# A hybrid of window attention, linear attention and a recurrence: the second image's channel blocks in the planner's list

## The chip, the cores and the metric

The kernel runs on one NeuronCore of a Trainium2 chip. A core has five engines that run their own instruction streams: TensorE (PE in the profile, with its weight loads as PEld), VectorE (DVE), ScalarE (ACT), GpSimd (POOL) and SyncE (SP). SP does no arithmetic here; it issues nearly all DMA transfers, in order. [...] The metric is device time in microseconds of one execution.

## The reference

The input is 16 images of 56 x 56 pixels with 128 channels, in float32. Layer 0 normalises each image by groups of channels and runs shifted window attention on 7 x 7 windows (64 windows per image, 4 heads of 32). Layer 1 takes each image as 3136 tokens, runs causal linear attention, and then a recurrence over the tokens. Cut to what matters:

```python
x = x + window_attention(_gn(x), w_qkv, pos_emb, w_out, b_out)  # 7x7 windows
t = _to_tokens(x)                                  # (16, 3136, 128)
t = t + linear_attention(_ln_t(t), W, b)           # causal, running k-v state
wx = batch_norm(_ln_t(t) @ ffn_W.T)                # mean and variance over all images
for i in range(3136):                              # one state per image
    y[:, i] = sigmoid(wx[:, i] + y[:, i - 1] @ V.T)
t = t + y
```

`_gn` needs the mean and variance of a whole image before its first window can be projected. The recurrence needs the statistics of all images, so it comes last.

## The kernel before

**Two parts.** The first part works through the images one after another and overlaps neighbouring ones. Its instruction order is computed by a small planner in the kernel. The second part, the recurrence, has an order written by hand (from about 1497 us on in the profiled execution).

**One image in the first part.** An image is loaded twice. `load` (L323 issues it) brings its tokens into `xt_buf`, tokens on partitions, in seven groups: six of 512 tokens and one of 64. `load_turned` brings the same image into `spare[0]` as four channel blocks of 32 channels, through `load_blocks` (L335); block q fills partitions 32q to 32q+31. Seven 32 x 32 block transposes on DVE (`turn_rows`, L683) turn `spare[0]` into channels on partitions in `xw_buf`; each reads all 128 partitions, so all four blocks. Seven `bn_stats` on DVE (L755) follow, then the group norm: two small matmuls (L784, L800), a few tiny DVE and POOL steps, and a wrap-around copy of the borders on POOL (L773, L774). The first image is turned by TensorE instead (L649), from `xt_buf`.

Then come eight rows of windows. A row is gathered and normalised by ACT (L851), projected (L864, L885), scored (L909, in 32-row matmuls), masked and reduced on DVE (L920, L932), shifted on POOL (L935), exponentiated on ACT (L945), summed on DVE (L949, L951), scaled on POOL (L954), transposed (L964, copied by ACT in L974) and multiplied with the values (L983, 32-row matmuls again).

After enough rows, the token groups: output bias on POOL (L1223), output projection (L1234, L1243), token norm (L1090 on DVE, L1097 to L1111 on POOL), a trip through DRAM that turns blocks (stored in L1058, read back in L1072, turned on DVE in L1139), features (L1269, L1279, L1288, L1292), values (L1317, L1326), products (L1372, L1382), keys (L1348), running state and outputs (L1401, L1404, L1412, copied by ACT in L1424), the residual (L1482, L1490), a second norm and the input of the recurrence (L1502, L1519).

**The planner.** Each piece of work is a step: an engine, a cost (how long the engine is held), a lag (when its users may start), a rank, the steps it comes after, and the buffers that it takes and gives back. `Plan.forwards` places steps engine by engine, taking the ready step of lowest rank; `Plan.backwards` does the same from the end and gives new ranks. `Plan.emit` alternates them 200 times, keeps the plan with the shortest planned span, and emits all steps in the order of their planned starts. So one changed step can change the order of everything. The steps exist only while the program is built: on the chip, an engine waits only where an instruction uses data or a buffer that another one is still working on.

**Around the change.** The steps of `load_turned` are on SP, with a cost of 2.4 and a lag of 12.0 for the images of index 1 and 2 and of 7.0 for the later ones. Each comes after `issued` (a step without instructions that stands for the loads of constants, with a lag of 19.0) and after the block before it, and all take the one buffer `spare`. The tokens of the image of index 2 are held back by small memsets on POOL (`touch`, L601), which come after the transposes of the second image.

## Time and profile before

| what | value |
|---|---|
| median of 3 runs | 1659.49 us (1656.48 to 1663.47) |
| profiled execution | 1664.5 us |
| its span | 1661.4 us |
| PE busy | 1615.4 us |
| DVE busy | 1398.1 us |
| POOL busy | 1272.0 us |
| ACT busy | 1183.5 us |
| moved by DMA | 322.03 MB, mean 194 GB/s |

The profile is of one execution. Its span is what the engines' records cover; the execution's own time is a little longer. Times within it are counted from the start of the span. A line in order of time gives the start, the length, engine, line, operation and tiles, how many instructions were merged, and in brackets how long the engine had been idle and what ended that. For a DMA on SP the length is that of issuing it. A busy PE need not be at its peak, since matmuls are pipelined.

### The profile page before, as it was taken

How to read it: one execution, taken by the hardware profiler on the slowest of the kernel's cores; microseconds unless marked ns; L12 is line 12 of the kernel's file. 1: busy time of each engine (PE TensorE's matmuls, PEld its weight loads, DVE VectorE, ACT ScalarE, POOL GpSimd, SP SyncE). 2: the span in 40 equal slices, each digit the busy share in tenths (PEclk: the TensorE clock that was granted, in tenths of full speed). 3: DMA queues.
4: the chain of work that ended last, by engine and by line, in shares of the span. 5: the costliest groups of instructions: out<-in, count | busy, mean ns of one | idle time of the engine just before them, and what ended most of it. 6: DMA issues, size and time to landing. Idle time of an engine off the chain costs nothing.

```text
span 1661.4 us, 63385 instructions
## 1 busy us (share of the span) xinstructions
PE 1615.4 (97%) x25458; PEld 1308.8 (79%) x25459; DVE 1398.1 (84%) x3044; ACT 1183.5 (71%) x3156; POOL 1272.0 (77%) x2154
## 2 busy tenths in 40 slices
PE   7899999999999999999999999999999999999997
PEld 6678787887878887878888778878888887876876
DVE  5779987897989888987979798978898786757997
ACT  5577776777777777777677777767677776766765
POOL 6788978897989898888989889878889786770000
PEclk9999999999999999999999999999999999999999
DMA  5486767677677768586766777776755655558999
GB/s 137 109 186 158 192 151 172 187 167 208 154 204 166 199 153 206 149 208 169 194 165 156 204 168 196 167 191 156 196 148 155 159 160 147 190 183 342 403 419 379
DMA packets 776720, 322.03 MB, mean 194 GB/s; under 512 B 400481, under 2 KB 760161, under 8 KB 774625
## 3 DMA queue, kind: packets, MB, share of 16 engines
q1 hardware_dynamic: 774832, 317.10, 69.9%
q8 instruction: 202, 3.31, 0.9%
q10 hardware_dynamic: 1584, 0.79, 0.2%
q14 instruction: 102, 0.83, 0.2%
HBM read 171.54 MB, written 146.24 MB: 191 GB/s over the span
## 4 chain that ended last, share of the span: by engine, by line
PE 69%; POOL 8%; DVE 7%; SPq 5%; DMA 5%; issue 3%; ACT 2%; DVEq 0%; POOLq 0%; ACTq 0%
PE bank L864 8%; PE bank L1269 8%; PE bank L885 5%; PE pair L909 5%; PE state_bank L1412 4%; PE pair L964 4%; PE pair L1401 4%; PE bank L1317 4%; PE pair L1404 4%; PE bank L1502 4%; PE bank L1372 4%; PE pair L983 4%; SPq L1072 4%; PE bank L1234 4%; PE z_buf L1785 2%
## 5 line engine op out<-in xcount | busy, mean ns | idle before, releaser
L954 POOL TENSOR_TENSOR p_buf<-p_buf,rc 128x784 f32<-128x784 f32 x128 | 194.4, 1519 | 42.7 <-DVE rc L951 14.2
L1269 PE MATMUL bank<-xnT,awc_sb 128*128 128x512 f32 (+1 forms) x448 | 212.9, 557 | 3.3 <-DVE xnT L1139 2.7
L935 POOL TENSOR_TENSOR s<-s,mx 128x784 f32<-128x784 f32 x128 | 192.2, 1502 | 30.8 <-DVE mx L932 28.5
L1279 ACT ACTIVATE r<-bank,bqk_neg 128x512 f32<-128x512 f32 (+1 forms) x224 | 143.4, 640 | 76.9 <-PE bank L1269 67.3
L1412 PEld LDWEIGHTS state_bank<-v_buf,k 128*128 128x128 f32 x768 | 125.4, 191 | 52.1 <-issue 26.7
L1292 DVE SCALAR_TENSOR_TENSOR f<-bank,bqk_one,r 128x512 f32<-128x512 f32 (+1 forms) x224 | 147.5, 658 | 12.6 <-ACT r L1288 12.1
L1412 PE MATMUL state_bank<-v_buf,k 128*128 128x129 f32 x768 | 155.4, 284 | 1.3 <-ACT state L1424 1.1
L974 ACT COPY pT<-pair 128x904 f32<-128x904 f32 x128 | 118.7, 927 | 51.0 <-PE pair L964 41.3
L1401 PE MATMUL pair<-state,f 128*128 128x129 f32 x768 | 153.1, 281 | 0.6 <-issue 0.6
L1424 ACT COPY state<-state_bank 128x129 f32<-128x129 f32 x384 | 107.0, 279 | 65.5 <-PE state_bank L1412 63.9
L1401 PEld LDWEIGHTS pair<-state,f 128*128 128x128 f32 x768 | 123.4, 192 | 37.0 <-issue 21.8
L920 DVE TENSOR_TENSOR s<-pair,wmask_sb 128x784 f32<-128x784 f32 x128 | 122.7, 958 | 34.2 <-PE pair L909 30.0
L909 PEld LDWEIGHTS pair<-kT,q_buf 32*49 32x49 f32 x8192 | 106.4, 121 | 41.9 <-issue 15.7
L949 DVE TENSOR_REDUCE sm<-p_buf 128x16 f32<-128x784 f32 x128 | 121.6, 950 | 18.6 <-ACT p_buf L945 18.3
L1223 POOL TENSOR_TENSOR xt_buf<-xt_buf,bout_sb 128x512 f32<-128x512 f32 (+1 forms) x112 | 129.1, 1158 | 10.7 <-DMA xt_buf<-in_x_dram 10.5
L1788 ACT ACTIVATE y_a<-z_buf,bsh 128x256 f32<-128x256 f32 (+1 forms) x218 | 103.0, 473 | 47.4 <-PE z_buf L1785 43.3
L1288 ACT ACTIVATE r<-r 128x512 f32<-128x512 f32 (+1 forms) x224 | 131.9, 589 | 2.4
L1785 PE MATMUL z_buf<-y_a,fvT_sb 128*128 128x256 f32 (+1 forms) x432 | 131.0, 389 | 0.4 <-ACT y_a L1788 0.4
L909 PE MATMUL pair<-kT,q_buf 32*49 32x49 f32 x8192 | 122.8, 206 | 2.8 <-issue 2.4
L964 PE MATMUL pair<-ident,p_buf 113*128 113x113 f32 x1024 | 120.9, 261 | 3.1 <-POOL p_buf L954 2.8
L964 PEld LDWEIGHTS pair<-ident,p_buf 113*128 113x128 f32 x1024 | 107.5, 142 | 20.5 <-issue 11.2
L932 DVE TENSOR_REDUCE mx<-s 128x16 f32<-128x784 f32 x128 | 121.5, 949 | 0.9
(170 smaller groups left out, 4697.1 us busy)
## 6 DMA issues: line engine op xcount, KB each, us to landing
x_d<-xt_buf SPq DMA_DIRECT2D x96, 256.0 KB, 2.6
xt_buf<-in_x_dram SPq DMA_DIRECT2D x93, 256.0 KB, 3.2
spare<-in_x_dram SPq DMA_DIRECT2D x60, 392.0 KB, 4.5
xs_d<-staged SPq DMA_DIRECT2D x15, 1568.0 KB, 6.9
xna_d<-spare SPq DMA_DIRECT2D x90, 256.0 KB, 2.7
xnk_d<-f SPq DMA_DIRECT2D x90, 256.0 KB, 3.0
xnf_d<-spare SPq DMA_DIRECT2D x90, 256.0 KB, 2.8
spare<-xna_d SPq DMA_DIRECT2D x256, 64.0 KB, 2.1
```

What stands on the lines that cost most here:

```text
L864: nc.tensor.matmul(d[key], wqkv_sb[:, j * P : (j + 1) * P], xk, start=True, stop=True)
L909: nc.tensor.matmul(sc[64 * hh : 64 * hh + WT, hp, w * WT : (w + 1) * WT], qT[r : r + HD, w * WT : (w + 1) * WT], d["kT"][r : r + HD, w * W ...
L935: nc.gpsimd.tensor_tensor(d["sf"], d["sf"], d["mx"].unsqueeze(2).to_broadcast([P, nb, WT]), ALU.subtract,)
L954: nc.gpsimd.tensor_tensor(prf, prf, d["rc"].unsqueeze(2).to_broadcast([P, nb, WT]), ALU.mult)
L964: nc.tensor.transpose(pt[:, hp, w2, 0:NQ2], pr[0:NQ2, hp, 2 * w2 : 2 * w2 + 2, :].rearrange("p w k -> p (w k)"), ident[0:NQ2, 0:NQ2],)
L1269: nc.tensor.matmul(d[f"p{j}"], awc_sb[:, j * P : (j + 1) * P], d["xT"][:, :nt], start=True, stop=True,)
L1279: nc.scalar.activation(d[f"r{j}"], d[f"p{j}"], AF.Relu, bias=bqk_neg[:, j : j + 1], scale=-1.0,)
L1288: nc.scalar.activation(d[f"r{j}"], d[f"r{j}"], AF.Exp, scale=-1.0)
L1292: nc.vector.scalar_tensor_tensor(d[key][:, :nt], d[f"p{j}"], bqk_one[:, j : j + 1], d[f"r{j}"], ALU.add, ALU.max,)
L1401: nc.tensor.matmul(to, chunk(d["f0"], cc), t["states"][c], start=True, stop=False)
L1412: nc.tensor.matmul(t["pd"], d["k"][:, cc, :], v1[:, cc, :], start=c == 0, stop=True, skip_group_check=True,)
L1785: nc.tensor.matmul(z, fvT_sb, y_prev, start=False, stop=True, skip_group_check=True)
```

## The change

The list of steps that a channel block comes after no longer holds the block before it, if the image is the second one (index 1). For all later images the list is as it was. All four blocks of the second image still come after `issued` and still take the same buffer.

```diff
                         2.4,
                         rank + q,
                         lambda q=q: load_blocks(b, spare[0], q),
-                        [issued, *parts[-1:]],
+                        [issued, *(parts[-1:] if b > 1 else [])],
                         takes=[buf],
                         lag=12.0 if b < 3 else 7.0,
                     )
```

## The prediction

> **What bounds the kernel now.** I read the page's first two parts, then busy time by stretches, then the instructions of SP, DVE and PE in order of time up to 110 us, and last what PE waits for. The page says which engine is full and whether it is full everywhere:

> ```profile
> PE 1615.4 (97%) x25458; PEld 1308.8 (79%) x25459; DVE 1398.1 (84%) x3044; ACT 1183.5 (71%) x3156; POOL 1272.0 (77%) x2154
> ...
> PE   7899999999999999999999999999999999999997
> ```

> PE has work in all slices but the first two and the last. Busy time by stretches puts numbers on it (columns: stretch, its length, then busy time and instructions of PE, weight loads, DVE, ACT and POOL; granted clock, DMA share, GB/s):

> ```profile
> 0.00:55.00 55.00, 44.95 (x851) 35.54 (x852) 31.13 (x53) 31.51 (x79) 39.76 (x57) 1.00 0.48 118
> 55.00:60.00 5.00, 3.50 (x142) 2.98 (x140) 3.32 (x5) 3.14 (x8) 4.10 (x9) 1.00 0.38 82
> 60.00:64.00 4.00, 3.63 (x12) 2.65 (x13) 1.74 (x7) 1.78 (x3) 3.75 (x8) 0.58 0.21 57
> 64.00:100.00 36.00, 32.03 (x500) 25.15 (x498) 31.22 (x71) 21.58 (x54) 26.48 (x51) 1.00 0.75 180
> 100.00:200.00 100.00, 98.48 (x1778) 79.91 (x1778) 92.69 (x206) 75.25 (x200) 89.88 (x143) 1.00 0.75 176
> 200.00:1400.00 1200.00, 1188.19 (x20148) 966.25 (x20148) 1028.51 (x2304) 876.93 (x2395) 1031.25 (x1738) 1.00 0.70 175
> ```

> The reader is to see that from 200 to 1400 us PE stands idle for 11.8 us in 1200 us: there the kernel is bound by PE's own work, which the change leaves as it is. What a change of the order can win lies in the fill: 10.1 us idle before 55, 1.9 from 55 to 64 (plus slow matmuls at clock 0.58), 4.0 from 64 to 100, 1.5 from 100 to 200.

> Now the loads themselves, on SP, and the first use of them on DVE:

> ```profile
> 11.73 0.43 SPq L335 DMA_DIRECT2D spare<-in_x_dram  x1
> 12.21 5.91 SPq L323 DMA_DIRECT2D xt_buf<-in_x_dram  x7
> 18.17 3.80 SPq L335 DMA_DIRECT2D spare<-in_x_dram  x2
> 48.11 0.39 SPq L1058 DMA_DIRECT2D xna_d<-spare  x1
> 50.52 2.02 SPq L1072 DMA_DIRECT2D spare<-xna_d  x4
> 52.58 0.43 SPq L335 DMA_DIRECT2D spare<-in_x_dram  x1
> ...
> 49.85 0.97 DVE L920 TENSOR_TENSOR s<-pair,wmask_sb 128x784 f32<-128x784 f32 x1 [3.59 <-PE pair L909]
> 68.16 1.16 DVE L683 STREAM_TRANSPOSE xw_buf<-spare 128x448 f32<-128x448 f32 x2
> ```

> Three blocks of the second image are issued by 22 us. The fourth stands behind work of the first image in SP's order and goes out at 52.58; it lands 4.3 us later (the median from issue to landing in that window), about 56.9. Its users on DVE come at 68.16, with no wait before them: they stand there because the planner put them there. Blocks two and three go out in one stretch of 3.80 us, though their landing takes 6.7 us: on the chip no block waits for another. So the change removes no wait of the chip. It removes three waits of 12 us from the planner's list, and everything follows from the order that the planner then writes.

> PE meanwhile runs dry, and the first matmul of the second image's windows is the one at 90.88:

> ```profile
> 58.45 0.94 PE L1234 MATMUL bank<-wout_sb,oT_buf 128*128 128x128 f32 x7 [0.90 <-issue]
> 60.37 1.81 PE L1269 MATMUL bank<-xnT,awc_sb 128*128 128x512 f32 x2 [0.98 <-DVE xnT L1139]
> 79.21 1.16 PE L1372 MATMUL bank<-f,f 128*128 128x128 f32 x8 [0.72 <-DVE f L1292]
> 90.88 0.82 PE L864 MATMUL bank<-oT_buf,wqkv_sb 128*128 128x392 f32 x2
> ```

> **The change part by part.** The built order of the changed kernel shows four moves.

> *SP.* All four blocks go out together right behind the constants, ahead of the seven loads of the second image's tokens. Three loads of 392 KB move before them: at the 250 GB/s or so of 20 to 22 us that delays the tokens by 4.7 us. The last of them now lands about 23 us; their first user on POOL starts at 31.62 without a wait, and DMA is silent from 26 to 32 us, so this costs nothing; without that cover it would cost 4.7 us. The third image's token loads, from 69.88 to 85.6 before, now stand before the read-back of the first normalised group (issued at 50.52 before), and wait on small POOL memsets that the order places after the softmax step which ran at 48.04. I put that read-back 2 us later; its user on DVE came at 59.53, some 5 us after landing, which covers it. The third image's blocks stay chained.

> [...]

> *DVE.* The seven transposes (L683, 0.61 us each), seven statistics (L755, 0.60) and the group-norm steps (1.0 together) move from 68 to 86 us up to the stretch from 36 to 58: 9.5 us. DVE's idle time there (lines with 2.60, 1.50, 1.45, 1.05, 3.59, 0.38 and 1.85 between 30 and 58 us) is 12.4 us, so most is hidden. Not all: walked through by these durations, the softmax maximum of row 3 ends 2.2 us later, but POOL, which uses it, is busy until 0.45 us after its old start; one round on, POOL's scaling of row 3 (52.16) starts 1.2 us late, and PE's transposes of it (53.73) with it. Bounds: 0 if all hides, 4.3 (seven transposes) if none of them does; I take **+1.2 us**, from the walk.

> *PE.* The order is the same through the transposes at 53.73. After it the second image's first projection is 14 groups of matmuls on instead of 44; I put it at 67 us instead of 90.9. From there window rows stand between the token groups, so the waits on DVE and ACT have other work to cover them: the 4.0 us of 64 to 100 go, **-4.0 us**. Bounds: -7.4 (with the 1.9 of 55 to 64 and the 1.5 after 100) and 0. The idle stretch at 57 to 60 stays, since the first image's rows are then spent and the second's not begun. With it stays the slow clock: L1269 takes 1.81 us at 60.37 against 1.02 elsewhere, granted clock 0.58 over 4 us, a loss of 1.7 us; I take 0, bounds -1.7 and +1.7.

> [...]

> *The order beyond 100 us.* All of it is rewritten. One countable thing: PE changes between the 32-row matmuls (L909, L983) and the full ones 406 times instead of 424. Across such a change a start-to-start step is 0.32 us where it is 0.22 otherwise (1408.67 to 1408.99 against 1412.47 to 1412.69). 18 x 0.10 = **-1.8 us**, bounds -3.6 and 0. What can't be counted is how many stalls the new order has. The 24 stretches of 50 us between 200 and 1400 idle 0 to 2.94 us each, mean 0.49, spread 0.82; so a sum over 24 scatters by 4.0, and the difference of two such plans by 5.7. I take 0; bounds -11.8 (no stall left) and +11.8 (twice as many). From 1500 us on the order is written by hand and stays.

> Sum: +1.2 - 4.0 - 1.8 = **-4.6 us**. The profiled execution took 1664.5 us (span 1661.4), 0.3% above the median of 1659.49; its span would become 1656.8, and from the median I get **1655 us**, 0.3% less.

> **The rivals.**
> 1. *The fill is lost again.* The inserted DVE work costs its whole 4.3 us against 4.0 and 1.8 won: 1658. For it: POOL is 88% busy from 20 to 40 us and DVE's idle time comes in pieces of 1 to 3 us.
> 2. *The new order is better throughout.* Fill and clock at their bounds without the part after 100 (-5.9, -1.7), changes -1.8, one spread of stalls -5.7: 1644. For it: DVE and POOL are idle for 14% of the time after 200. Against: only 1% of PE is left to win there.
> 3. *Slower: late feedback in the steady part.* One such place before: PE waits 2.7 us for DVE at 1384.9, and clock 0.5 follows for 3.4 us, 4.4 us in all.

> ```profile
> 1387.56 1.34 PE L1317 MATMUL bank<-awc_sb,xnT 128*128 128x128 f32 x8 [2.69 <-DVE xt_buf L1243]
> ```

> Each further such place costs 4.4 us; three outweigh the gain by 8.6 us, which is where it decides: 1668. For it: SP issues in order, and the new order puts more loads with waits before read-backs. Against: only two stretches of 24 hold such a place now.

> **How the numbers follow.** What can be told from no change is about 0.5%, 8.3 us. Chances: forecast 0.40, rival 1 0.15, rival 2 0.27, rival 3 0.18. Faster by over 0.5% is rival 2 and the forecast's lower edge (0.05): 0.32; slower is rival 3: 0.18; the rest 0.50. The likeliest case alone spans 1649 to 1661. The range reaches to both outer rivals and a little beyond the slower one, whose stalls have no ceiling: 1643 to 1671.

> **What would show it.** Right: L683 on DVE near 37 to 46 us, the second image's L864 before 70 us, PE idle from 64 to 100 under 1.5 us, 200 to 1400 near 12. Wrong: L1269's first pair later than 62 us, PE idle in the steady part over 20 us, or clock below 1.00 in more than the two stretches there.

## The result and the profile after

The changed kernel takes 1665.91 us (median of 12 runs, 1660.24 to 1674.23) against 1656.97 us for the kernel before (12 runs, 1655.40 to 1663.47). The ratio is 1.0048, with an interval from 1.0031 to 1.0066. It is 0.48% slower where 0.3% faster was forecast; the time lies inside the range, the direction is wrong. The profiled execution took 1666.84 us, with a span of 1665.1.

The page of the changed kernel again says what is full:

```profile
PE 1615.3 (97%) x25459; PEld 1306.4 (78%) x25459; DVE 1398.8 (84%) x3044; ACT 1185.8 (71%) x3156; POOL 1271.2 (76%) x2154
...
PE   7999999999999999999999999999999999999997
```

PE is busy for 1615.3 us, as before (1615.4). The work is the same; only the idle time and the slow clock can have moved. Busy time by stretches, with the columns of before (stretch, length, then PE, weight loads, DVE, ACT, POOL; granted clock, DMA share, GB/s):

```profile
0.00:55.00 55.00, 45.13 (x885) 35.90 (x889) 38.02 (x71) 31.93 (x79) 40.48 (x66) 1.00 0.63 153
55.00:60.00 5.00, 4.29 (x128) 3.58 (x118) 4.28 (x8) 2.79 (x8) 4.75 (x9) 1.00 0.73 140
60.00:64.00 4.00, 4.00 (x143) 2.91 (x142) 2.34 (x7) 3.13 (x6) 3.83 (x9) 1.00 0.22 66
64.00:100.00 36.00, 35.07 (x639) 27.84 (x638) 29.59 (x60) 27.84 (x70) 30.87 (x45) 1.00 0.55 120
100.00:200.00 100.00, 97.05 (x1633) 78.27 (x1633) 90.02 (x204) 70.70 (x192) 87.88 (x152) 1.00 0.77 182
200.00:1400.00 1200.00, 1184.39 (x20057) 960.34 (x20055) 1023.62 (x2290) 874.89 (x2382) 1024.56 (x1718) 0.99 0.69 174
...
1460.00:1500.00 40.00, 35.96 (x249) 29.45 (x248) 22.24 (x68) 24.79 (x77) 29.64 (x67) 1.00 0.54 180
```

The fill did what was forecast: idle time of PE from 64 to 100 us fell from 4.0 to 0.9 us, from 55 to 64 from 1.9 to 0.7, and the slow clock at 60 to 64 is gone (1.00 after 0.58). The loss comes later: PE idles 3.0 us instead of 1.5 from 100 to 200, 15.6 instead of 11.8 from 200 to 1400 (at clock 0.99), 4.0 instead of 2.6 from 1460 to 1500.

The instructions of SP, DVE and PE that answer to those shown of before:

```profile
11.80 6.49 SPq L335 DMA_DIRECT2D spare<-in_x_dram  x4
18.34 5.79 SPq L323 DMA_DIRECT2D xt_buf<-in_x_dram  x6
...
36.57 0.64 DVE L683 STREAM_TRANSPOSE xw_buf<-spare 128x448 f32<-128x448 f32 x1
...
53.50 0.99 PE L964 MATMUL pair<-ident,p_buf 113*128 113x113 f32 x8 [0.41 <-POOL p_buf L954]
...
59.34 1.12 PE L1269 MATMUL bank<-xnT,awc_sb 128*128 128x512 f32 x2
...
66.71 0.93 PE L864 MATMUL bank<-x_buf,wqkv_sb 128*128 128x392 f32 x2
```

All four blocks go out at 11.80; the first transpose on DVE starts at 36.57 instead of 68.16, the second image's first projection at 66.71 instead of 90.88 (67 was forecast).

Where the time went is seen in PE's idle times. In order of time, with what ended them in brackets, five of them look like this:

```profile
384.38 0.27 PE L1412 MATMUL state_bank<-v_buf,k 128*128 128x129 f32 x1 [1.60 <-issue]
...
567.14 0.49 PE L1234 MATMUL bank<-wout_sb,oT_buf 128*128 128x128 f32 x2 [0.41 <-issue]
...
750.54 0.94 PE L1372 MATMUL bank<-f,f 128*128 128x128 f32 x6 [1.52 <-issue]
...
931.99 0.50 PE L1372 MATMUL bank<-f,f 128*128 128x128 f32 x3
934.61 1.44 PE L1372 MATMUL bank<-f,f 128*128 128x128 f32 x5 [2.12 <-issue]
935.95 2.05 PE L1269 MATMUL bank<-xnT,awc_sb 128*128 128x512 f32 x2
...
1026.56 0.85 PE L909 MATMUL pair<-kT,q_buf 32*49 32x49 f32 x55
1029.11 0.33 PE L909 MATMUL pair<-kT,q_buf 32*49 32x49 f32 x9 [1.70 <-issue]
```

At 1026.56 PE does 55 of 64 equal matmuls of one line on one pair of tiles, stands still for 1.70 us, and does the other 9. Nothing that the engines exchange lies between them, and the releaser is "issue": PE waits for no other engine. The five sum to 7.36 us. After the longest, the pair of L1269 takes 2.05 us where 1.02 is usual: the clock was granted at 0.5 for 3.4 us. The profile of before has three such places, 2.44 us:

```profile
118.84 0.57 PE L909 MATMUL pair<-kT,q_buf 32*49 32x49 f32 x30 [0.69 <-issue]
...
200.43 0.68 PE L909 MATMUL pair<-kT,q_buf 32*49 32x49 f32 x41 [0.72 <-issue]
...
1112.95 0.28 PE L909 MATMUL pair<-kT,q_buf 32*49 32x49 f32 x2 [1.03 <-issue]
```

In each of the five of the changed kernel PE resumes 8 to 9 us behind the issue of the same transfer, the store of the recurrence's input (L1537, 1568 KB). Of the three of before, the last two end 9.5 and 8.3 us behind such a store; the first comes before any store is issued. DMA around the last one, first from just before the store's issue to just before the gap, then in the 1.6 us after it (a row of busy tenths in 40 slices, the packets, and then the queue that carries PE's instructions, in the second stretch only):

```profile
DMA  5889999999999999999999999999999999999999
...
DMA packets 3212, 2.05 MB, mean 321 GB/s; under 512 B 697, under 2 KB 3212, under 8 KB 3212
```

```profile
q8 instruction: 1, 0.02, 3.6%
```

The store was issued here:

```profile
1020.08 0.45 SPq L1537 DMA_DIRECT2D xs_d<-staged  x1
1020.62 4.96 SPq L1072 DMA_DIRECT2D spare<-xna_d  x4
```

Queue q8 moves 202 packets of 16 KB in the whole execution, on the median one in 7.6 us. That the queue is PE's can be counted: 50918 matmuls and weight loads over 202 packets are 252 to a packet, and in all five places PE resumes 1.3 to 1.5 us after such a packet ends. At each of them PE has begun 256 instructions for every packet of q8 that has ended, plus 193 (matmuls, weight loads and semaphore instructions together; at the last place 34497 instructions and 134 packets). The same sum, with the same 193, holds at all nine idle times of PE over 0.3 us without a releaser that the first profiles of the two kernels have between 100 us and 40 us before the recurrence (four before, five after). So at these nine places PE stands still where a block of 256 instructions ends and the next one isn't there yet. PE waits for its own instructions too (up to 2.12 us here), not only for data and buffers as the part on the planner has it.

From 1020.0 to 1026.4, while the store and the read-backs issued behind it fill DMA, no packet of q8 appears. The one before started at 1013.50, the next at 1026.67. Spacing alone does not show that it is late (14.0 us from 819.3 on go without a gap), but PE's own progress does: the packet starts 4.3 us after PE began the block before the one that it brings, and the median of this profile is 0.95 us. At the five places it is 1.2, 2.7, 4.4, 4.4 and 4.3 us; at the first of them PE also used up a block in 2.0 us. Packets that start within 9 us behind a store have a median of 2.4 us, the others 0.9. So the theory: **a block of PE's own instructions comes too late, because a large store is ahead of it.**

### The profile page after: what moved, and what is told of

The parts are those of the page before. It is cut to its first block, busy times and chain, and to the rows that moved or that the text cites. A ratio compares the mean times of both kernels' runs of the same rounds, so it can differ in the third digit from the quotient of the medians.

```text
span 1665.1 us, 63371 instructions
## 1 busy us (share of the span) xinstructions
PE 1615.3 (97%) x25459; PEld 1306.4 (78%) x25459; DVE 1398.8 (84%) x3044; ACT 1185.8 (71%) x3156; POOL 1271.2 (76%) x2154
## 4 chain that ended last, share of the span: by engine, by line
PE 74%; DVE 7%; POOL 6%; DMA 4%; SPq 4%; issue 3%; ACT 1%; DVEq 0%; POOLq 0%; ACTq 0%
PE bank L1269 9%; PE bank L864 8%; PE bank L885 6%; PE pair L909 5%; PE state_bank L1412 5%; PE bank L1317 5%; PE pair L964 5%; PE pair L1401 5%; PE bank L1372 5%; PE pair L1404 5%; PE pair L983 4%; PE bank L1502 4%; PE bank L1234 4%; SPq L1072 3%; PE z_buf L1785 2%
## 5 line engine op out<-in xcount | busy, mean ns | idle before, releaser
L1269 PE MATMUL bank<-xnT,awc_sb 128*128 128x512 f32 (+1 forms) x448 | 213.6, 559 | 3.4 <-DVE den L1474 1.1
L1292 DVE SCALAR_TENSOR_TENSOR f<-bank,bqk_one,r 128x512 f32<-128x512 f32 (+1 forms) x224 | 148.3, 662 | 23.3 <-ACT r L1288 21.3
L920 DVE TENSOR_TENSOR s<-pair,wmask_sb 128x784 f32<-128x784 f32 x128 | 122.6, 958 | 32.5 <-PE pair L909 25.2
L909 PEld LDWEIGHTS pair<-kT,q_buf 32*49 32x49 f32 x8192 | 105.5, 120 | 36.9 <-issue 14.7
L909 PE MATMUL pair<-kT,q_buf 32*49 32x49 f32 x8192 | 121.6, 206 | 1.7 <-issue 1.7
L945 ACT ACTIVATE p_buf<-s 128x784 f32<-128x784 f32 x128 | 113.0, 884 | 12.9 <-POOL s L935 12.4
```

The costliest lines, as they stand in the source:

```text
L909: nc.tensor.matmul(sc[64 * hh : 64 * hh + WT, hp, w * WT : (w + 1) * WT], qT[r : r + HD, w * WT : (w + 1) * WT], d["kT"][r : r + HD, w * W ...
L1269: nc.tensor.matmul(d[f"p{j}"], awc_sb[:, j * P : (j + 1) * P], d["xT"][:, :nt], start=True, stop=True,)
L1292: nc.vector.scalar_tensor_tensor(d[key][:, :nt], d[f"p{j}"], bqk_one[:, j : j + 1], d[f"r{j}"], ALU.add, ALU.max,)
```

## The experiments

The kernel before took between 1656.6 and 1664.6 us from session to session, on different chips. So times are compared within a session, or as ratios to the kernel before of the same session.

**Theory and rivals.** Theory S (store): the rewritten order puts more places where PE runs through a block of instructions during the store. Rival B: the burst of four loads itself harms something. Rival F: late feedback, read-backs through DRAM that reach DVE late, as the prediction's third rival had it. Rival Q: the store hurts only through its place in SP's queue. Rival C: chance of a single profile.

### The loads together, in the order of before

```diff
+            if b == 1:
+                for p in parts:
+                    p.early = parts[0]
...
-        for s in sorted(self.steps, key=lambda s: start[s.n]):
+        for s in sorted(self.steps, key=lambda s: start[(s.early or s).n]):
```

The planner works as before; only the emission puts the second image's four blocks together. Beside it the kernel before ran as its own control.

> The kernel before, unchanged, as a second look at where it stalls. All theories: same time as before within 0.2%. If the stalls of its first profile (PE waiting 2.7 us at 1385 us) are part of its order, they come again at the same place; if they are chance, they are elsewhere or gone, and the execution is some 4 us shorter than the first profiled one.

> The order of before is kept for every engine, with one thing moved: the second, third and fourth channel block of the second image are issued on SP right behind the first (as in the changed kernel). So the early transfer is tried without a new order. Order theory (the loss comes from the rewritten order): same as before, within 2 us. Rival, early burst (the 1.2 MB ahead of the second image's tokens is itself late for someone): slower by 4 to 9 us, with POOL waiting for the tokens near 31 us.

The control: 1657.02 us, ratio 1.000 (0.9985 to 1.0015). PE's wait of 2.7 us for DVE near 1385 us is there again at the same instruction, with 1.97 us and without a slow clock behind it; the gaps within groups are there again too, with 2.77 us in sum. The loads together: 1656.99 us, 1.000 (0.9988 to 1.0012). Order on SP and busy time by stretches of that kernel:

```profile
11.76 6.67 SPq L336 DMA_DIRECT2D spare<-in_x_dram  x4
```

```profile
64.00:100.00 36.00, 31.89 (x497) 25.18 (x497) 31.25 (x72) 22.98 (x56) 27.79 (x56) 1.00 0.80 192
```

The four loads go out as in the changed kernel, and it neither costs nor gains: PE still idles 4.1 us from 64 to 100, since the users stand where they stood. Rival B falls: what the change does, it does through the order.

### The store in four parts

```diff
-            def emit():
+            def emit(i=0):
+                m = slice(NJ * i // 4, NJ * (i + 1) // 4)
                 nc.sync.dma_start(
-                    xs_d[:, :, b].rearrange("m p k n -> p m (k n)"),
-                    t["xsT"].rearrange("p (m k) n -> p m (k n)", k=KB),
+                    xs_d[m, :, b].rearrange("m p k n -> p m (k n)"),
+                    t["xsT"].rearrange("p (m k) n -> p m (k n)", k=KB)[:, m],
                 )
...
+            s.later = [(2.0 * i, lambda i=i: emit(i)) for i in range(1, 4)]
```

The other parts are emitted 2, 4 and 6 us behind the first on the planner's scale; the order of all other instructions stays. Both kernels got it.

> The order of the changed kernel is kept, but the store of each image's recurrence input (1568 KB in one transfer) goes out in four parts, planned 2 us apart. Store theory (behind this large store PE's instruction blocks arrive late, and the new order has PE run through its instructions fastest just there): the gaps of PE within a group of matmuls, 7.4 us in the changed kernel, fall under 3 us, the dips of the clock that follow them go, and the time falls by 6 to 10 us to that of before or below. Rival, read-backs (the new order leaves DVE waiting for blocks that come back through DRAM): no change, within 2 us, since these waits stay.

> The same split of the store with the order of before. Store theory: a gain of 0 to 3 us, since the gaps of PE within a group are 2.4 us there. Read-back theory: no change, within 2 us.

The changed kernel with the divided store takes 1657.61 us, ratio 1.0003 (0.9989 to 1.0016): the 0.48% are gone. Busy time by stretches, and PE at the places of the 1.60 and the 1.70 us gap:

```profile
64.00:100.00 36.00, 35.07 (x642) 27.84 (x626) 29.59 (x59) 27.61 (x69) 30.36 (x44) 1.00 0.54 120
200.00:1400.00 1200.00, 1188.66 (x20240) 964.56 (x20239) 1030.93 (x2307) 880.28 (x2397) 1031.78 (x1733) 1.00 0.70 175
```

```profile
381.39 0.27 PE L1416 MATMUL state_bank<-v_buf,k 128*128 128x129 f32 x1 [0.18 <-issue]
...
1021.21 0.95 PE L913 MATMUL pair<-kT,q_buf 32*49 32x49 f32 x64
```

At 1021.21 the 64 matmuls run through; at 381.39 the 1.60 us gap is 0.18. No gap above 0.3 us within a group is left between 100 us and 40 us before the recurrence, and no stretch of slow clock in the steady part. From 200 to 1400 PE idles 11.3 us instead of 15.6. The fill's gain stays. Against PE's progress, the packets of the five places now start at -0.9, 2.2, 3.1, 1.2 and 1.6 us, each of them earlier than before (-0.9 is 0.9 us before PE began the block ahead). Theory S holds for the changed kernel, and rival F, which had the time unchanged, falls: PE's waits for DVE over 0.3 us stay at 9.7 us, and the loss is gone. Not all of the 7 us of gaps became time: from 100 us to 40 us before the recurrence PE idles 14.4 us against 18.6 and 17.3 in the two profiles without the division, mainly since waits for ACT grew to 3.2 us from 0 and 1.0.

The kernel before with the divided store takes 1660.40 us, 1.0014 (1.0001 to 1.0028), where 0 to 3 us less were expected: a miss. It had only 2.4 us of such gaps to lose. One of 0.59 is left, that near 117 us, which comes before the first store (issued at 189.6 us) and so has another cause; and one wait of PE for DVE, which waits for a read-back, grew to 3.75 us (1.97 in the control). Dividing isn't a gain in itself.

### The changed kernel again, and the store on ACT's queue

```diff
             def emit():
-                nc.sync.dma_start(
+                nc.scalar.dma_start(
                     xs_d[:, :, b].rearrange("m p k n -> p m (k n)"),
```

> The changed kernel, unchanged, as a second look beside the runs that follow. All theories: 0.3% to 0.7% slower than before. Store theory: gaps of PE within a group again behind the same stores (those at 375, 742, 926 and 1020 us), 5 to 9 us in all. If these gaps are chance, they sit behind other stores or sum up to less than 4 us.

> The order of the changed kernel, with the large store of each image issued on ACT's queue instead of SP's. It is as large and as early as before. Store theory, with the DMA engines themselves as the place (a late instruction block waits for an engine that is busy with the store): the gaps within groups stay at 5 to 9 us, and the time stays within 3 us of the changed kernel. If the place is SP's queue alone, the gaps fall under 3 us and the read-backs that stand behind the store on SP land sooner too: 5 to 10 us faster.

The changed kernel again: 1664.68 us, 1.0038 (1.0020 to 1.0055). PE after the gaps:

```profile
381.51 0.27 PE L1412 MATMUL state_bank<-v_buf,k 128*128 128x129 f32 x1 [1.61 <-issue]
...
746.71 0.94 PE L1372 MATMUL bank<-f,f 128*128 128x128 f32 x6 [1.64 <-issue]
...
930.67 0.82 PE L1372 MATMUL bank<-f,f 128*128 128x128 f32 x5 [1.84 <-issue]
...
1025.49 0.33 PE L909 MATMUL pair<-kT,q_buf 32*49 32x49 f32 x9 [1.66 <-issue]
```

Four of the five gaps are back at the same instructions, even at the same matmul of the group (9 left of 64), in another session: 6.75 us in sum; the fifth, 0.41 us before, is 0.27. They belong to the program, not to the execution. Rival C falls for the gaps. Not for the slow clock: its 3.4 us stretches come at 272, 385, 935 and 1030 us in the first profile, and at 141 and 933 in this one.

With the store on ACT's queue the gaps stay (five, 6.12 us; four at the old places, while the longest is gone and one of 1.66 us came at 1405.8, 24 us behind a store), so it isn't SP's queue that makes them: Q falls. But the time is 1678.82 us, 1.0118 (1.0094 to 1.0142), 14.1 us over the changed kernel, where at most 3 us were expected: a miss. What SP waits for, and what DVE and PE wait for near 932 us in that kernel:

```profile
SPq L323 <- DMA xs_d<-staged: 8.7, 1, 8.7
```

```profile
936.93 0.71 DVE L1139 STREAM_TRANSPOSE xfT<-spare 128x512 f32<-128x512 f32 x1 [9.25 <-DMA spare<-xnf_d]
...
938.28 2.08 PE L885 MATMUL bank<-wqkv_sb,oT_buf 128*128 128x128 f32 x8 [6.54 <-DVE v_buf L1326]
```

From one queue to another the next load on SP now waits 8.7 us until the store has landed, and the read-back behind it on SP is late for DVE, and DVE for PE. SP waits over 1.5 us for a store's landing behind 12 of the 15 stores; in the two profiles with the store on SP's queue it does so behind none and one. Waits of PE for DVE over 0.3 us sum to 20.2 us instead of 9.7 and 7.8. That is rival F's mechanism, here made by the edit.

### Another order, by chance

```diff
-HOP = 0.06
+HOP = 0.061
```

`HOP` is a constant of the planner's costs. A thousandth on it gives another order of the same work.

> The kernel before with another order by chance: the planner's allowance for a step from engine to engine is 0.061 instead of 0.060, which changes nothing on the chip but the order from the first images on. Luck theory (any new order scatters by several us, and the order of before was a good one): 2 to 12 us slower than before, with no common cause. If orders are about as good as each other: within 3 us.

> The changed kernel with the same other allowance of 0.061. If the change itself costs (not only this one order of it), it is 6 to 10 us slower than its counterpart without the change. Luck theory: it lies anywhere from 8 us faster to 8 us slower than that counterpart, and PE's idle time from 64 to 100 us is again near 1 us instead of 4.

The kernel before in this second order: 1661.39 us, 1.0020 (1.0006 to 1.0034), with four gaps within groups, 6.38 us. With the change: 1650.24 us, 0.9946 (0.9925 to 0.9967), with three, 2.45 us. So here the change *wins* 11.2 us, more than the 8 us that the expectation allowed either way. A third order, 0.062:

> The kernel before in a third order (HOP 0.062). Theory that the order is drawn by chance: 1652 to 1664, by the two orders seen (1657 and 1661). No rival number: it is the other half of the next run.

> The changed kernel in the third order. Theory (fill gain of 4 us in every order, the rest by chance with a spread of about 6 us): 1643 to 1665, PE idle from 64 to 100 us below 1.5 us; against the run before it the difference lies between -15 and +8. Rival, that the change itself brings late instruction blocks: over 5 us of gaps and slower than the run before it by 5 us or more, as in the first order.

1658.69 us (0.9965, 0.9948 to 0.9982) without the change, 1657.30 (0.9949, 0.9929 to 0.9970) with it: the intervals overlap. PE idles 4.2 us from 64 to 100 us without and 0.1 with the change. The fill's gain is there in every order; the change as a whole is worth from +9 to -12 us.

### The second order, store whole and divided

> The kernel before in the second order (HOP 0.061), its store of the recurrence's input issued as four parts 2 us apart. Unsplit it took 1661.39 us with 6.38 us of gaps of PE within groups of matmuls. Theory that the instruction blocks are late behind the undivided store: these gaps fall below 1 us and the time falls to about 1656 (1653 to 1659). Rival, that the gaps belong to the order and not to the store: gaps stay at 5 us or more and the time at 1660 to 1664.

> The changed kernel in the second order (HOP 0.061) with the divided store. Undivided it took 1650.24 us with 2.45 us of such gaps. By the store theory at most these 2.45 us can be won: 1648 to 1651. Rival: dividing adds waits of DVE for read-backs, as in the kernel before in its first order (3.4 us slower): 1652 to 1656.

The kernel before took 1664.58 us in the session of these two, so they are read by their ratios. Before with the divided store: 1661.51 us, 0.9976 (0.9961 to 0.9991), gaps 3.66 us where under 1 was expected: a miss. Changed with the divided store: 1653.47, 0.9930 (0.9906 to 0.9954), no gaps within groups (one of 0.84 us is left between two groups). The four variants were then run in one session:

> The kernel before in the second order again, now on one chip with its three variants below. Before it had 6.38 us of gaps of PE within groups of matmuls. Theory (instruction blocks late behind large stores): the same gaps at 291 and 750 us, 5 to 7 us in sum; this is the base of the next run.

> The same with the store in four parts. On another chip two gaps of 1.35 and 2.31 us stayed, at the same places. Store theory with several stores together as a second source: 3 to 6 us faster than the run above on the same chip, gaps 2 to 4 us. Rival, that the division is worth nothing in this order: within 2 us of the run above.

> The changed kernel in the second order again: 8 to 12 us faster than the kernel before in that order on the same chip (11.2 and, with the divided store, 8.0 were measured), gaps 2 to 3 us. Rival, that the 11.2 was a chance of that job: within 5 us.

> The same with the divided store: the gaps go (0 to 1 us), so 1 to 4 us faster than the run above. Rival, that what is won in gaps comes back as waits of DVE for read-backs or in the last 40 us before the recurrence (4.1 against 2.2 us idle there): same or up to 3 us slower.

| second order, one session | time, us | ratio to the kernel before (interval) | gaps within groups, us |
|---|---|---|---|
| without the change, store whole | 1665.77 | 1.0011 (0.9997 to 1.0026) | 5.59 |
| without the change, store divided | 1659.79 | 0.9977 (0.9962 to 0.9992) | 3.42 |
| with the change, store whole | 1653.81 | 0.9934 (0.9915 to 0.9954) | 4.07 |
| with the change, store divided | 1651.48 | 0.9927 (0.9909 to 0.9944) | 0 |

Busy time from 200 to 1400 us, in the order of the table, each from the profile of its kernel:

```profile
200.00:1400.00 1200.00, 1187.98 (x20170) 964.60 (x20168) 1030.15 (x2306) 880.60 (x2393) 1032.96 (x1732) 1.00 0.70 175
```

```profile
200.00:1400.00 1200.00, 1189.24 (x20242) 965.60 (x20246) 1032.26 (x2309) 880.43 (x2395) 1033.55 (x1733) 1.00 0.70 175
```

```profile
200.00:1400.00 1200.00, 1190.02 (x20225) 966.64 (x20226) 1032.09 (x2316) 883.73 (x2401) 1036.83 (x1734) 1.00 0.70 175
```

```profile
200.00:1400.00 1200.00, 1194.31 (x20296) 970.85 (x20295) 1036.58 (x2328) 885.19 (x2407) 1040.74 (x1744) 1.00 0.70 175
```

PE idles 12.0, 10.8, 10.0 and 5.7 us there: each edit takes some away. The medians gain by both in this order, the division 6.0 us alone and 2.3 with the change (these two intervals overlap, so the 2.3 isn't shown), the change 12.0 alone and 8.3 with the division. The rival that the 11.2 was chance falls; so does, without the change, the one that the division is worth nothing.

The miss has a place. PE at 740 to 751 us, without the change, store whole, then divided; then with the change, whole, then divided:

```profile
750.28 0.20 PE L909 MATMUL pair<-kT,q_buf 32*49 32x49 f32 x1 [1.92 <-issue]
```

```profile
747.93 0.20 PE L913 MATMUL pair<-kT,q_buf 32*49 32x49 f32 x1 [3.02 <-issue]
```

```profile
746.37 0.30 PE L983 MATMUL pair<-pT,v 49*32 49x49 f32 x10 [1.36 <-issue]
```

```profile
743.38 0.81 PE L987 MATMUL pair<-pT,v 49*32 49x49 f32 x64
```

In the second fence the gap stays though the store is divided. There PE runs two rows of 64 small matmuls one behind the other, 256 instructions with their weight loads in about 2 us, a whole block. Nor is the store near in the first fence, where it is whole: it was issued at 735.69 and landed at 742.97, so the gap ends 14.6 us behind the issue, and the packet that ends it started 1.7 us after PE began the block before. Here PE uses up a block faster than the next one comes, with no store on the way. So this case shows two ways to such a gap, a packet that starts late behind a large store, which the first order shows, and a run of small matmuls as long as a block. What other transfers add was not tested.

The version with both edits in the second order has the lowest ratio: 0.7% under the kernel before, measured in two sessions. Its interval overlaps that of the change alone in this order.

## Why the prediction was wrong

**DVE's insertion, +1.2: too high by 1.2.** The transposes of row 3 start at 53.50 instead of 53.73; PE's idle time up to 55 us is 9.9 us in the first profile and 10.1 in the second, against 10.1 and 9.9 before. DVE's idle pieces took the 9.5 us in whole.

**The fill, -4.0: right.** 64 to 100 gave 3.1 us, 55 to 64 another 1.2, which the prediction had in the bound: -4.3 in sum. In the first order every kernel with the change idles 0.9 us from 64 to 100. The slow clock at 60 us went, as the lower bound had it (-1.7). But the control shows it at 32 instead of 61 us, and with the change it is at 59 to 61 us again in the second and third orders: it moves from execution to execution, and that it was gone here is luck.

**Fewer tile changes, -1.8: not seen.** PE's busy time up to the recurrence, less the 1.7 us that each stretch of slow clock costs (3.4 us at 0.5), is 1460.2 and 1458.5 us in the two profiles of before and 1460.0 and 1459.7 in those of after: a difference of +0.5, not -1.8. What was counted as a gain has another side: fewer changes mean longer runs of small matmuls. Runs that go from L909 straight into L983, or back, are 53 instead of 44.

**The order beyond 100 us, "I take 0": the step that failed.** It took the stalls of the new order for chance around those of the old one. They are fixed by the order: the gaps come back at the same instructions. From 100 us to 40 us before the recurrence PE idles 18.6 and 17.3 us in the two profiles of after, 14.0 and 13.3 in those of before: +4.3. In the last 40 us it is 4.9 and 4.9 against 2.5 and 2.5: +2.4. So this term measured **+6.7**, inside its bounds of 11.8 and a little over the one spread of 5.7. The whole of the +4.3 is in the gaps within groups (7.36 and 6.75 against 2.44 and 2.77, +4.45). The waits for DVE did not grow: 9.7 and 7.8 against 8.0 and 8.0. The 2.4 us of the last 40 were not tested by themselves; in the second order they went the other way (2.2 us with, 5.0 without the change), in the third the same way (5.2 with, 3.4 without), so they go with the order drawn; their cause stays open.

Why the first order of the changed kernel meets the store so often can be told in part. In the 8 us behind each of the 15 stores PE starts 315 instructions on the mean against 269 before, and 13 of 15 stores have more than 256, the size of a block, against 6 of 15. Many of those 13 have no gap, though; which of them stall isn't settled.

**The sum.** -4.3 and +6.7 are +2.4; with half a stretch of slow clock more (0.9) and the 0.5 of busy time, +3.8. The recurrence starts 3.7 us later on the mean (1501.8 and 1497.0, against 1497.8 and 1493.6). So the profiles account for what they show. They show less than the medians do (+8.9 in the first session, +6.8 in the second), because both profiled executions of before happened to lie 3 to 8 us above their median. The profile with the loads together, which has the order of before but for three loads and was taken of an execution near the median (1655.43 us), shows what the other two had in excess: there PE idles 29.5 us up to the recurrence, 5.0 less than the mean after the change, and no slow clock comes before it, where the two profiles after the change have three stretches on the mean (5.1 us). Its recurrence starts 10.4 us earlier and its span is 8.7 us shorter. For the same reason the base was off: 1659.49 was the median of 3 runs, 12 give 1656.97.

**The rivals.** The third had the sign and nearly the time (1668), and the wrong mechanism: late feedback doesn't grow. Its price of 4.4 us a place was too high: 1.5 to 2.1 us for a gap, and 1.7 more where the slow clock follows. The second rival (1644) was the nearest in the second order (1650.24). Nothing in the profile of before told which of them the planner would draw. The scatter of orders has no sign, so the chances of the two rivals, 0.27 and 0.18, had no reason to differ by more than the fill's 4 us make.

**What would show it.** Three of the four marks for the mechanism came; idle time from 200 to 1400 near 12 did not, it is 15.6 and 15.2. Of the marks for wrong, a late first pair of L1269 (59.34) and idle time over 20 did not come; clock below 1.00 in more than two stretches came in the first profile, with four, and not in the second.

**What the rows leave open.** No packet of q8 starts between 1020.0 and 1026.4 us, the 6 us of the store, and the next one starts 4.3 us after PE began the block before, against 0.95 on the median. Whether DMA serves that packet late or the request for it comes late, no trace here shows.

The clock fell to 0.5 for 3.4 us after gaps of 1.60, 2.12 and 1.70 us, not after 1.52 in the same profile, and in the next profile after 1.84, not after 1.61, 1.64 and 1.66. So the length of a gap does not tell it alone. In each of the first profiles of the two kernels the slow stretches (from 61, 289, 1388 and 1617 us on before, from 272, 385, 935 and 1030 us on after) start whole multiples of 3.41 us apart. Divided into pieces of 3.41 us in step with them, from 25 us on and without the last 15 us of the span, the two profiles have eight pieces in which PE was busy for 0.84 to 1.81 us, and a slow stretch began behind each of them; in all others PE was busy for 1.82 us or more, and none began behind them. The gap of 1.52 us lies for the most part in a piece with 2.12 us. So the place of a gap in these pieces may count too. A gap at the same instruction has a slow stretch behind it in one profile (385, 1030 us) and none in the next.

## What to carry to other kernels

Where a planner writes the order, a small edit is two things: what it says, which could be walked through and came within 1 us of its forecast in three orders (3.1, 3.3 and 4.1 us less idle time from 64 to 100, 4.0 forecast), and a new draw of everything else: the two together moved the time by anything from +9 to -12 us. Judge such an edit over several orders, and search over orders for its own sake. On an engine that is 97% busy, look for idle time within groups of equal instructions with no releaser. Here it pointed to PE's own instruction stream, since all nine idle times over 0.3 us without a releaser in the first profiles of the two kernels, from 100 us to 40 us before the recurrence, came at whole blocks of 256 instructions. A large transfer a few us ahead (1568 KB, issued 8 to 9 us before the gap's end) is then the first suspect, a long run of small matmuls (128 of them at the gap of 3.02 us) the second. Try to divide that transfer (1.0003 instead of 1.0048 for the changed kernel, 1.0014 for the one before), but leave it on the queue where other transfers are ordered behind it (1.0118 on ACT's).
